# Four image layers on one core: ends of attention blocks in pieces, a first load in smaller pieces, a setup in steps

## The chip, the cores and the metric

The kernel runs on one core of a Trainium2 chip, in one launch. The metric is device time in microseconds; three runs of the kernel before give a median of 2654.44 us (2654.04 to 2654.82). A profiled execution of it spans 2652.8 us. A core has five engines that work side by side, each through its own queue in order: TensorE (PE in the profile: matrix products and transposes; PEld are its weight loads), VectorE (DVE), ScalarE (ACT), GpSimd (POOL) and SyncE (SP, which here only issues transfers). They wait for each other through semaphores. Operands lie in SBUF, products arrive in PSUM, a small memory that TensorE writes and VectorE and ScalarE read.

## The reference

The input is four images of 64 x 64 positions with 64 channels, float32 (n = 4096 positions per image). Four layers follow each other; all of them are done in float32.

```python
# layer 0: self-attention over positions; attn is used transposed
q, k, v = (x @ Wq + bq, x @ Wk + bk, x @ Wv + bv)          # each (b, n, 64)
attn = softmax(q @ k^T, axis=-1)                            # (b, n, n)
x = gamma * einsum("bmn,bmc->bnc", attn, v) + x

# layer 1: gated convolution block
y = dw3x3(layernorm(x) @ pw1 + b)                           # 256 channels
y = y1 * y2                                                 # halves of the channels
y = y * (mean(y over positions) @ sca + b)
x = x + (y @ pw2 + b) * beta
z = layernorm(x) @ pw3 + b
x = x + ((z1 * z2) @ pw4 + b) * gamma

# layer 2: attention along the other reading of the same memory, no weights
xf = x.reshape(b, 64, n)
x = softmax(xf @ xf^T) applied to xf, plus x

# layer 3: non-local block with batch norm over all images
f = softmax((x @ theta) @ (x @ phi)^T)                      # inner width 32
w_y = (f @ (x @ g)) @ w_W + w_b
out = x + gamma * (w_y - mean(w_y)) * rsqrt(var(w_y) + 1e-3) + beta
```

(In layer 2 the code writes `x.shape` as `B, C, H, W`, so it is the first image axis, of length 64, that plays the channels, and the 4096 others are the summed positions; the kernel follows that.) The mean and variance of layer 3 go over all images, so the output can't begin before the last of them has been projected.

## The kernel before

**Tiles.** `X` holds all four images in SBUF, each as 128 partitions (two halves of the image times 64 channels) by 2048 columns. PSUM is shared out as three tiles `ps` of 128 x 1024 (`new_ps`), which take scores, projections and transposes, and two tiles `acc` of 128 x 512 (`new_acc`), which gather sums over many products. Six tiles `e` of 128 x 2048 (`new_e`) hold exponentials. A tile that is asked for when all of its kind are in use waits until the oldest one has been read for the last time.

**Order.** The order on TensorE, VectorE and ScalarE is the order in which the program is written; nothing reorders it. `run()` (L1495) goes through a list of items. An item is one `scores` call of an attention layer: 32 of layer 0 per image, 32 of layer 2, 64 of layer 3. `at(i, fn)` adds a function that runs after the scores of item i: usually the `products` of an earlier item. So TensorE always has the scores of the next item to do while ScalarE forms the exponentials of the last. Two lanes, `conv` (setup of the weights, then layer 1) and `misc` (loads, projections, layer openings), are generators; each `yield us` says how long a step is counted for, and after the scores and again after the products of an item a lane takes as many steps as fit into the item's count (3.6 us, 4.6 us and 1.0 us a tick for layers 0, 2 and 3). Layer 3 of image b follows layer 2 of image b + 1.

**Start.** `fetch_x(0)` (L738) loads the first image in four transfers, two on SyncE's queue and two on ScalarE's; the small vector `bq` comes next on SyncE's queue. `fold_qk` multiplies the two query and key weights into one matrix `wq` and a bias `bqk`; `load_x(0)` (L920) turns the image by transposes (L924), eight per PSUM tile, with a copy to `X` (L925); `project0` (L971) makes `q` (L997, L1002) and `v` (L1007, L1009). Then come the scores of layer 0 (L1031).

**Setup of weights.** `setup()` (L879) folds the layer norm's gain, shift and mean into the weights of layer 1: eight one-column products (L891) and their sums, then for each of two matrices a scaling on VectorE (L901), a product with `cmat` (L902) and a copy. All of it but the first step is one lane step.

**Query step of images 1 to 3.** `project0` with "once" forms four products in a `ps` tile (L982); VectorE adds the bias to both halves (L990), 64 partitions x 1024 each, and a transfer doubles each half (L993).

**norm.** In layer 1 ScalarE squares the image (L1082), and after a `yield 4.0` TensorE averages the image and its squares over channels (L1088).

**Layer 2.** `scores(n)` (L1245) and exp with the sum of each row (L1253); `products(n)` (L1262) runs one item after its scores and needs both `acc` tiles when n is a multiple of 8.

**Layer 3.** `scores(n)` writes two `ps` tiles (L1361), ScalarE two exponentials (L1367). `products(n)` runs two items later. It multiplies `e` by `gx` into the accumulator `y` (L1389), and adds up `e` for the softmax's denominators: on VectorE into `esum` (L1383, L1385), or, where `mc % 10 == 9`, by TensorE with a matrix of ones straight into the accumulator `z` (L1378). Here n = 32 nb + mc: there are two blocks of 32 items, nb = 0 and 1. After a block, `yz` takes a copy of `y` (L1395), and `totals` adds `esum` into `z` (`sums`, L1399), inverts `z` as exp(-ln z) on ScalarE (L1410, L1411) with one Newton step on VectorE (L1412 to L1414), and scales `yz`. `close` multiplies `yz` with the output weights in a new `ps` tile (`project`, L1419), adds the bias on ScalarE (L1432) and takes statistics on VectorE (L1434). `totals` comes four items after the block's last scores (two for the second block of images 0 and 1), `close` eight. The last block of the last image has its own end, `close_last` (L1436 on).

**Output.** `finish()` (L1536) joins the statistics, scales, adds and transposes (L1607) and stores in pieces; before the last piece's copy, `check_sums` (L1635) counts on VectorE whether all sums of the softmaxes lie in a range. If not, a slower general path would run; with these inputs it doesn't.

Of the kernel before, what the change touches and what calls it, by code (L numbers as in the profile page):

```python
# [691 lines left out]
def fast_path(ctx: ExitStack, tc: tile.TileContext, a: dict, out: bass.AP, bad):  # L692
# [44 lines left out]

    def fetch_x(b, queues):  # L738
# [4 lines left out]
        for g in range(2):  # L743
            for p in range(2):
                (queues[p] if b == 0 else queues[g]).dma_start(
                    out=t[64 * p : 64 * p + 64, bass.ts(g, 8)], in_=src[p, :, bass.ts(g, 8)]
                )
# [131 lines left out]
    def setup():  # L879
# [7 lines left out]
        for i, (w_, sh, bi) in enumerate(  # L887
            ((pw1, "L1_conv_ln1_b", "L1_conv_pw1_b"), (pw3, "L1_conv_ln2_b", "L1_conv_pw3_b"))
        ):
            for r in range(2):  # L890
# [3 lines left out]
                )  # L894
            nc.vector.tensor_add(
                pwb[:, i, :], ps[:, 2 * i : 2 * i + 2], vec[:, col[bi] : col[bi] + 2]
            )

        ps = new_ps()
        for i, (w_, g) in enumerate(((pw1, "L1_conv_ln1_g"), (pw3, "L1_conv_ln2_g"))):  # L900
            nc.vector.tensor_scalar_mul(w_, w_, V(g))  # L901
            mm(ps[:, 512 * i : 512 * i + 256], cmat, w_, start=True, stop=True)  # L902
            nc.vector.tensor_copy(w_, ps[:, 512 * i : 512 * i + 256])
        for i in range(4):
# [5 lines left out]
        nc.vector.tensor_mul(resb[:, 0:1], V("L1_conv_pw2_b"), V("L1_conv_beta"))  # L910
        nc.vector.tensor_mul(resb[:, 1:2], V("L1_conv_pw4_b"), V("L1_conv_gamma"))
        yield 3.0
# [7 lines left out]
    def load_x(b):  # L920
        for g in range(2):
            ps = new_ps()
            for i in range(8):
                nc.tensor.transpose(ps[:, bass.ts(i, 128)], rows_x[b][:, 8 * g + i, :], ident)  # L924
            (nc.vector.tensor_copy if g else nc.scalar.copy)(X[:, b, bass.ts(g, 1024)], ps)  # L925
            yield 3.0
# [9 lines left out]
    def at(i, fn):  # L936
        due.setdefault(i, []).append(fn)
# [33 lines left out]
    def project0(b):  # L971
# [5 lines left out]
        for j, w in once if b else ((0, "q"), (0, "v"), (1, "q"), (2, "q"), (1, "v"), (3, "q")):  # L977
            ps = new_ps()
            if w == "once":
# [7 lines left out]
                for o in range(2):  # L987
                    own, other = slice(64 * o, 64 * o + 64), slice(64 - 64 * o, 128 - 64 * o)
                    n = bass.ts(2 * j + o, 512)
                    nc.vector.tensor_scalar_add(  # L990
                        qs[own, :, n], ps[own, :].rearrange("p (s n) -> p s n", s=2), bqk[own, :]
                    )
# [84 lines left out]
    def norm(x, y):  # L1077
# [5 lines left out]
        yield 4.0  # L1083
# [147 lines left out]
    def layer2(b):  # L1231
# [51 lines left out]
        for n in range(32):  # L1283
            items.append((lambda n=n: scores(n), 4.6))
            at(first + n + 1, lambda n=n: products(n))
# [17 lines left out]
    wys, early = {}, []  # L1303

# [44 lines left out]
    def layer3(b):  # L1349
# [3 lines left out]
        def scores(n):  # L1353
# [12 lines left out]
            for kp in range(2):  # L1366
                act(e[:, bass.ts(kp, 1024)], tiles[kp], AF.Exp)  # L1367

        def products(n):
# [4 lines left out]
            if mc % 10 == 9 or (last and n >= 62):  # L1374
                if mc == 9:
                    st["z"] = new_acc("accz")
# [330 lines left out]
```

## Time and profile before

Busy time of each engine in the 2652.8 us span:

| engine | busy us | share |
|---|---|---|
| TensorE (PE) | 2612.8 | 98% |
| ScalarE (ACT) | 1718.6 | 65% |
| VectorE (DVE) | 1348.6 | 51% |
| GpSimd (POOL) | 16.4 | 1% |

The dearest groups by line: exponentials of layer 0 (L1036) 517.1 us, of layer 2 (L1253) 517.0, of layer 3 (L1367) 496.0; the sums of layer 3 on VectorE (L1385) 490.4; the scores of layer 0 (L1031) 475.5 and layer 2 (L1245) 469.8; the products of layer 2 (L1262) 468.5 and layer 0 (L1056) 467.4; scores and products of layer 3 (L1361, L1389) 309.5 and 272.0.

Rows of a timeline give the start in us, the length, the engine, the line, the operation, output <- inputs with their shapes, the count, and in brackets the idle time of the engine before it with what ended it. Rows of the waits name engine and line, then what was waited for, the total in us, the number of times, and the longest. Ends of matmuls are modelled and overlap with the next ones; the distance from one start to the next is the safer measure. Matmuls that sit in different parts of the array run side by side, so a group's count says little of its time.

### The profile page before, as it was taken

To read this page: it belongs to the slowest core of one execution; us is meant where nothing else is said; L and a number is where in the kernel's file an instruction comes from. 1 tells how busy PE (TensorE), PEld (TensorE's weight loads), DVE (VectorE), ACT (ScalarE), POOL (GpSimd) and SP (SyncE) were. 2 spreads that over 40 slices of the span, in tenths; PEclk is the share of its full clock that TensorE was granted. 3 is DMA by queue.
4 is the path that set the end of the run, shared out by engine and by line. 5 is a ranking of instruction groups with operands and counts; after the bars stand their busy time and mean duration, and the time that the engine had idled before them with its cause. 6 is when DMAs were issued, how large, how long until landed. Compare 5 with 4: busy or idle time off the path is not lost.

```text
span 2652.8 us, 50797 instructions
## 1 busy us (share of the span) xinstructions
PE 2612.8 (98%) x22421; PEld 830.2 (31%) x22421; DVE 1348.6 (51%) x1555; ACT 1718.6 (65%) x2787; POOL 16.4 (1%) x66
## 2 busy tenths in 40 slices
PE   8999999999999999999999999999999999999998
PEld 3333233333323323333333322243322333322223
DVE  3232386633876338621672148800068600098997
ACT  4555655656566565666656668756578755578886
POOL 2000000000000000000000000000000000000000
PEclk9999999999999999999999999999999999999999
DMA  3000000001000100010010000010000010010002
GB/s 73 1 17 1 17 8 10 1 17 25 9 1 1 32 17 1 1 33 17 1 33 17 17 1 1 2 33 1 17 1 2 1 33 1 1 33 2 1 1 66
DMA packets 24282, 36.46 MB, mean 14 GB/s; under 512 B 3725, under 2 KB 12150, under 8 KB 24054
## 3 DMA queue, kind: packets, MB, share of 16 engines
q1 hardware_dynamic: 23141, 32.03, 5.5%
q8 instruction: 178, 2.92, 0.5%
q0 software_dynamic: 672, 0.56, 0.1%
q10 hardware_dynamic: 240, 0.54, 0.1%
q14 instruction: 51, 0.41, 0.1%
HBM read 4.80 MB, written 4.19 MB: 3 GB/s over the span
## 4 chain that ended last, share of the span: by engine, by line
PE 93%; DVE 4%; ACT 2%; issue 0%; DMA 0%; SPq 0%; DVEq 0%; ACTq 0%
PE acc L1056 17%; PE acc L1262 17%; PE ps L1031 17%; PE ps L1245 16%; PE ps L1361 10%; PE acc L1389 8%; PE ps L1118 2%; DVE tg L1385 2%; PE accz L1378 1%; ACT e L1253 1%; PE ps L1209 1%; PE ps L1186 1%; PE ps L1088 1%; PE ps L1340 1%; PE ps L1007 0%
## 5 line engine op out<-in xcount | busy, mean ns | idle before, releaser
L1036 ACT ACTIVATE e<-ps 128x1024 f32<-128x1024 f32 x512 | 517.1, 1025 | 338.1 <-PE ps L1031 225.8
L1253 ACT ACTIVATE e<-ps 128x1024 f32<-128x1024 f32 x512 | 517.0, 1025 | 305.0 <-PE ps L1245 304.9
L1367 ACT ACTIVATE e<-ps 128x1024 f32<-128x1024 f32 x512 | 496.0, 1022 | 85.4 <-PE ps L1361 78.3
L1385 DVE TENSOR_TENSOR tg<-tg,e 128x2048 f32<-128x2048 f32 x214 | 490.4, 2292 | 24.7 <-ACT e L1367 5.7
L1031 PE MATMUL ps<-X,q 64*64 64x512 f32 x4096 | 475.5, 599 | 7.6 <-DVE q L990 4.1
L1245 PE MATMUL ps<-ko 64*64 64x512 f32 x4096 | 469.8, 591 | 2.2 <-ACT ko L1227 1.6
L1262 PE MATMUL acc<-e,X 64*64 64x512 f32 x4096 | 468.5, 591 | 2.6 <-DVE inv L1412 1.6
L1056 PE MATMUL acc<-e,vq 128*64 128x512 f32 x2048 | 467.4, 598 | 0.0
L1063 DVE SCALAR_TENSOR_TENSOR yv<-acc,gam,yv 128x512 f32<-128x512 f32 x224 | 167.8, 750 | 322.6 <-PE acc L1056 311.7
L1157 DVE SCALAR_TENSOR_TENSOR y<-pad,vec,y 128x1024 f32<-128x1024 f32 x240 | 308.1, 1284 | 8.1 <-ACT pad L1141 1.0
L1361 PE MATMUL ps<-tg,ph 32*64 32x512 f32 x4096 | 309.5, 613 | 1.4 <-DVE tg L1329 0.5
L1389 PE MATMUL acc<-e,tg 128*32 128x512 f32 x2048 | 272.0, 603 | 1.5 <-ACT yz L1395 1.5
L1245 PEld LDWEIGHTS ps<-ko 64*64 64x64 f32 x4096 | 157.7, 132 | 288.1 <-issue 195.4
L1262 PEld LDWEIGHTS acc<-e,X 64*64 64x64 f32 x4096 | 159.1, 133 | 278.7 <-issue 263.3
L1031 PEld LDWEIGHTS ps<-X,q 64*64 64x64 f32 x4096 | 143.2, 133 | 323.7 <-issue 224.8
L1056 PEld LDWEIGHTS acc<-e,vq 128*64 128x64 f32 x2048 | 136.0, 136 | 315.1 <-issue 294.4
L1270 DVE TENSOR_TENSOR ph<-ph,acc 128x512 f32<-128x512 f32 x16 | 11.0, 688 | 379.6 <-ACT ph L1269 379.6
L1361 PEld LDWEIGHTS ps<-tg,ph 32*64 32x64 f32 x4096 | 79.5, 129 | 218.7 <-issue 143.2
L1389 PEld LDWEIGHTS acc<-e,tg 128*32 128x32 f32 x2048 | 43.5, 108 | 202.3 <-issue 196.3
L1253 ACT ACTIVATION_READ_ACCUMULATOR e<-ps 128x1 f32 x512 | 106.1, 207 | 0.0
L1036 ACT ACTIVATION_READ_ACCUMULATOR e<-ps 128x1 f32 x512 | 106.0, 207 | 0.0
L1141 ACT ACTIVATE pad<-ps,pwb 128x512 f32<-128x512 f32 x64 | 44.6, 697 | 45.7 <-PE ps L1118 39.0
(193 smaller groups left out, 939.9 us busy)
## 6 DMA issues: line engine op xcount, KB each, us to landing
xn<-t SPq DMA_DIRECT2D x64, 128.0 KB
ph<-tg SPq DMA_DIRECT2D x64, 128.0 KB
ko<-ko SPq DMA_DIRECT2D x16, 256.0 KB
xr<-in_x_dram SPq DMA_DIRECT2D x14, 256.0 KB
q<-q SPq DMA_DIRECT2D x12, 256.0 KB
out_dram<-o SPq DMA_DIRECT2D x5, 512.0 KB
out_dram<-o SPq DMA_DIRECT2D x6, 256.0 KB
xr<-in_x_dram ACTq DMA_DIRECT2D x2, 256.0 KB
```

What stands on the lines that cost most here:

```text
L1031: mm(ps[64 * c : 64 * c + 64, bass.ts(r, 512)], m.q[rows_, 128 * t + 64 * c : 128 * t + 64 * c + 64], x[rows_, bass.ts(g, 512)], start=Tru ...
L1036: act(es[g // 2][:, bass.ts(g % 2, 1024)], ps, AF.Exp, bias=SHIFT0, accum_out=zs[:, g : g + 1],)
L1056: mm(accs[g][64 * r : 64 * r + 64, :], vq, es[half][:, 1024 * g + 512 * r : 1024 * g + 512 * r + 512], start=t == 2 * p, stop=t == 2 * p + 1,)
L1063: stt((x if p == 15 else m.y)[:, cols], accs[g], gam0, (m.y if p else x)[:, cols], ALU.mult, ALU.add,)
L1157: stt(y1, win, wt, y1, ALU.mult, ALU.add)
L1245: mm(ps[64 * c : 64 * c + 64, bass.ts(r, 512)], m.ko[rows_, 128 * jb + 64 * c : 128 * jb + 64 * c + 64], m.ko[rows_, bass.ts(2 * ib + r, 5 ...
L1253: act(es[n, jb], ps, AF.Exp, bias=SHIFT2, accum_out=m.zs[:, jb, ib : ib + 1])
L1262: mm(acc[r][64 * c : 64 * c + 64, :], xw[rows_, jb, :], es[n, jb][rows_, bass.ts(c, 512)], start=jb == 0, stop=jb == 31,)
L1361: mm(tiles[kp][64 * c : 64 * c + 64, bass.ts(i, 512)], m.ph[rows_, 128 * mc + 64 * c : 128 * mc + 64 * c + 64], m.th[rows_, bass.ts(nb, 51 ...
L1367: act(e[:, bass.ts(kp, 1024)], tiles[kp], AF.Exp)
L1385: nc.vector.tensor_add(esum, esum, e)
L1389: mm(st["y"][32 * k : 32 * k + 32, :], m.gx[:, mc, :], e[:, bass.ts(k, 512)], start=mc == 0, stop=mc == 31,)
```

## The change

It has eight edits, each meant to take a wait out of TensorE's way or to spread a lump of work:

1. The first image is loaded in six transfers (quarters, quarter, half) and transposed in three steps, so that the first products can begin on its first quarter.
2. The setup of weights is cut into seven lane steps, and the work inside is regrouped: all small products, then VectorE, then both large products.
3. In the query step of images 1 to 3, the second half's bias goes to ScalarE.
4. norm yields 5.0 instead of 4.0 after the squares.
5. In layer 2 of images 2 and 3, the first products run two items after their scores instead of one.
6. Layer 3: TensorE takes the sums at mc = 13, 20 and 27 (and 29 from n = 61 on) instead of 9, 19 and 29.
7. Layer 3: at five of the eight block ends (all but the second blocks of images 0, 1 and 3), `spread` puts the end into single items: Ln and Exp in two halves each, the Newton step later, the projection in two halves that reuse the accumulator `z` instead of a `ps` tile, the bias in four pieces. In the item where `yz` is copied, the second exponential is held back until after the copy.
8. `check_sums` moves behind the last store.

```diff
+    parts = ((0, 4), (4, 8), (8, 16)), ((0, 8), (8, 16))
...
-        for g in range(2):
+        for lo, hi in parts[b > 0]:
             for p in range(2):
-                (queues[p] if b == 0 else queues[g]).dma_start(
-                    out=t[64 * p : 64 * p + 64, bass.ts(g, 8)], in_=src[p, :, bass.ts(g, 8)]
-                )
+                queues[p].dma_start(out=t[64 * p : 64 * p + 64, lo:hi], in_=src[p, :, lo:hi])
...
+        for i, (_, _, _, bi) in enumerate(folds):
             nc.vector.tensor_add(
                 pwb[:, i, :], ps[:, 2 * i : 2 * i + 2], vec[:, col[bi] : col[bi] + 2]
             )
+        for w_, g, _, _ in folds:
+            nc.vector.tensor_scalar_mul(w_, w_, V(g))
+        yield 5.0
         ps = new_ps()
-        for i, (w_, g) in enumerate(((pw1, "L1_conv_ln1_g"), (pw3, "L1_conv_ln2_g"))):
-            nc.vector.tensor_scalar_mul(w_, w_, V(g))
+        for i, (w_, _, _, _) in enumerate(folds):
             mm(ps[:, 512 * i : 512 * i + 256], cmat, w_, start=True, stop=True)
+        for i, (w_, _, _, _) in enumerate(folds):
             nc.vector.tensor_copy(w_, ps[:, 512 * i : 512 * i + 256])
...
+        yield 5.0
...
-                    nc.vector.tensor_scalar_add(
-                        qs[own, :, n], ps[own, :].rearrange("p (s n) -> p s n", s=2), bqk[own, :]
-                    )
+                    src = ps[own, :].rearrange("p (s n) -> p s n", s=2)
+                    if o:
+                        act(qs[own, :, n], src, AF.Identity, bias=bqk[own, :])
+                    else:
+                        nc.vector.tensor_scalar_add(qs[own, :, n], src, bqk[own, :])
...
             act(sq[i], x[:, bass.ts(i, 1024)], AF.Square)
-        yield 4.0
+        yield 5.0
...
-            at(first + n + 1, lambda n=n: products(n))
+            at(first + n + (2 if n == 0 and b > 1 else 1), lambda n=n: products(n))
...
-            for kp in range(2):
-                act(e[:, bass.ts(kp, 1024)], tiles[kp], AF.Exp)
+            for fn in small.get((first + n, "PE"), []):
+                fn()
+            act(e[:, 0:1024], tiles[0], AF.Exp)
+            held.append(lambda: act(e[:, 1024:2048], tiles[1], AF.Exp))
+            if not (mc == 1 and (nb or last)):
+                held.pop()()
+            for fn in small.get((first + n, "ACT"), []):
+                fn()
...
-            if mc % 10 == 9 or (last and n >= 62):
-                if mc == 9:
+            if mc in (13, 20, 27 if n < 61 else 29) or (last and n >= 62):
+                if mc == 13:
                     st["z"] = new_acc("accz")
...
                 nc.scalar.copy(st["yz"][:, 0:512], st["y"])
+                if held:
+                    held.pop()()
...
+        def project_half(nb, jj):
+            if jj == 0:
+                open_wy(nb)
+            for s in range(2):
+                k = 2 * s + jj
+                mm(
+                    st["z"][64 * s : 64 * s + 64, :], wo[32 * k : 32 * k + 32, :],
+                    st["yz"][32 * k : 32 * k + 32, 0:512], start=True, stop=True,
+                )
...
+        def spread(n):
+            nb = n // 32
+            at(first + n + 4, sums)
+            for m, kind, fn in (
+                (5, "ACT", lambda: invert(slice(0, 256))), (6, "ACT", lambda: invert(slice(256, 512))),
+                (7, "ACT", lambda: invert2(slice(0, 256))), (8, "ACT", lambda: invert2(slice(256, 512))),
+                (9, "ACT", lambda: newton(nb)),
+                (12, "PE", lambda: project_half(nb, 0)), (12, "ACT", lambda: take(nb, 0, 0)),
+                (13, "ACT", lambda: take(nb, 0, 1)),
+                (14, "PE", lambda: project_half(nb, 1)), (14, "ACT", lambda: take(nb, 1, 0)),
+                (15, "ACT", lambda: take(nb, 1, 1)),
+            ):
+                small.setdefault((first + n + m, kind), []).append(fn)
...
-                at(first + n + (2 if n == 63 and b < 2 else 4), lambda n=n: totals(n // 32))
-                at(first + n + 8, lambda n=n: close(n // 32))
+                spread(n)
...
-                check_sums(mv)
...
+        check_sums(mv)
```

## The prediction

> **What bounds the kernel now.** I read the busy shares first, then the waits of TensorE, then TensorE's timeline at each place the diff touches.
>
> ```profile
> PE 2612.8 (98%) x22421; PEld 830.2 (31%) x22421; DVE 1348.6 (51%) x1555; ACT 1718.6 (65%) x2787; POOL 16.4 (1%) x66
> PE ps L1031 <- DVE q L990: 4.1, 2, 3.1
> PE acc L1262 <- DVE inv L1412: 1.6, 2, 0.8
> PE ps L1088 <- ACT sq L1082: 1.6, 1, 1.6
> PE acc L1389 <- ACT yz L1395: 1.5, 5, 0.3
> PE acc L875 <- DMA bq<-in_L_conv_bq_dram: 1.2, 1, 1.2
> ```
>
> TensorE is the bound: 40.0 us of the 2652.8 us span are not its work. A part of the change can win only what it takes out of these 40, plus matmuls that run slowly after a gap; each matmul that it adds is paid in full. The wait rows (total, times, longest) name what the edits aim at. They are small, so each is priced in its own stretch.
>
> Timeline of TensorE in the setup of weights (start, length, count, idle before):
>
> ```profile
> 45.66 0.60 PE L891 MATMUL ps<-vec,pw 64*128 64x1 f32 x4
> 47.24 0.57 PE L891 MATMUL ps<-vec,pw 64*128 64x1 f32 x4 [0.98 <-issue]
> 48.39 0.67 PE L902 MATMUL ps<-pw,cmat 128*128 128x256 f32 x2 [0.57 <-issue]
> 49.84 0.81 PE L902 MATMUL ps<-pw,cmat 128*128 128x256 f32 x2 [0.78 <-DVE pw L901]
> 50.58 5.19 PE L1031 MATMUL ps<-X,q 64*64 64x512 f32 x32
> 55.70 0.65 PE L1056 MATMUL acc<-e,vq 128*64 128x512 f32 x2
> ```
>
> Three gaps, and then 32 matmuls in 5.12 us that take 3.59 elsewhere.
>
> The same at a block end of layer 3:
>
> ```profile
> 2476.62 1.06 PE L1389 MATMUL acc<-e,tg 128*32 128x512 f32 x8 [0.31 <-ACT yz L1395]
> 2477.62 1.11 PE L1361 MATMUL ps<-tg,ph 32*64 32x512 f32 x16
> 2478.77 1.06 PE L1399 MATMUL accz<-tg,ones 128*32 128x512 f32 x8
> 2486.94 1.63 PE L1361 MATMUL ps<-tg,ph 32*64 32x512 f32 x16
> 2488.40 1.09 PE L1419 MATMUL ps<-yz,wo 32*64 32x512 f32 x8
> 2489.41 1.07 PE L1389 MATMUL acc<-e,tg 128*32 128x512 f32 x8
> ```
>
> To see: one wait of 0.31, the sums (L1399), one scores group of 1.63 instead of 1.11, the projection (L1419) in 1.01 to the next start. Then the start of layer 2 on image 2:
>
> ```profile
> 1710.27 1.04 PE L1399 MATMUL accz<-tg,ones 128*32 128x512 f32 x8
> 1711.60 1.07 PE L1262 MATMUL acc<-e,X 64*64 64x512 f32 x2 [0.30 <-ACT yz L1395]
> 1713.49 3.23 PE L1262 MATMUL acc<-e,X 64*64 64x512 f32 x27 [0.82 <-DVE inv L1412]
> ```
>
> **What the Trainium skill says.** (1) "TensorE: Matmul & The Clock Gate", What's actually happening: the array runs at half rate until a window of about 3.4 us was busy, and falls back after an idle one. The trace agrees: after the 3.15 us gap at 400.80, the 128-column matmuls of L1007 start 0.21 us apart until 408.6, then 0.11. (2) The same page, Part 3, The mechanism: matmuls in different tiles of the array run side by side. So a group costs the length of one, however many share it: L1419 holds 4 products in 1.01 us (2488.40 to 2489.41), L1186 only 2, also in 1.01 (1152.11 to 1153.12). (3) "ScalarE: Activation LUTs", What ACT_TABLE_LOAD costs: an ACTIVATE costs 186 ns, or 280 with a bias operand, plus 0.833 ns a column, and neighbours overlap by 93 ns. The trace has 0.375 us for 256 columns (L1440), 0.60 for 512, 1.02 for 1024. Cutting one of 512 into two of 256 costs ScalarE about 0.15 us more.
>
> **The change, part by part.**
>
> Setup of weights: from 45.66 to 55.70 are 10.04 us. After: eight L891 at 0.11 with a tail, 0.95; four L902 at 0.21 warm, 0.95; scores 3.59, with no gap between, as VectorE works while other matmuls run. 10.04 − 5.49 = **−4.5**.
>
> Query step of later images (L990): the second half goes from VectorE to ScalarE. At 396.5 VectorE has two such halves (1.28 each) in its queue, one before and one as the last; with one of each gone, the slot that L1031 waits for comes some 2.0 us earlier, and the gap of 3.15 becomes 1.15. Then most of the window is busy and L1118 (1.45 to the next start, not 0.95) and ten L1007 (0.21, not 0.11) stay warm: 0.5 + 1.0. At 666.63 the other gap, 0.98, loses 0.9, since the ScalarE half (about 1.0, as a 1024-column ACTIVATE) starts at once. ScalarE is busy 4.9 of 7.2 us in such an item, so it hides the half. −4.4; I take **−4.0**.
>
> norm, yield 4 to 5: a lane tick in layer 2 is 4.6 us, so with 4.0 the squares and the matmuls that read them can fall into one tick, as at 1159.40 (gap 1.62; and the 8 matmuls take 1.93 to the next start, not 0.99, as the second square trickles in). With 5.0 the reading step comes a tick later there: **−2.5**. All later steps of layer 1 shift by about half an item, with other meetings that I can't price: bounds 0 and −2.6.
>
> First products of layer 2 one item later, on two images: from 1710.27 to the third following scores at about 1723.7 are 13.4 us, where 0.96 + 3 × 3.59 = 11.7 are work. Loss 1.7. After, ScalarE still has the copy, Ln and Exp (0.59, 0.60, 0.63) ahead of the next exps, which costs the fourth score group some 0.2. 2 × 1.5 = **−3.0**. It must hold one item more of e, 6 of 6 buffers, which just fits.
>
> Range checks behind the last store: TensorE's last group and the last copy no longer have the VectorE checks (2641.37 to 2643.57) ahead of them; the last store goes about 0.7 earlier: **−0.6**. The checks then run under the store's transfer.
>
> First image in pieces: the first transposes start about 1 us sooner, but the projection waits for bq, whose transfer stands behind the image in SyncE's queue and lands at 10.1 either way. The four transposes for columns 512 to 1023, until now done under that wait, come after it: 4 × 0.21 = 0.85 later, part of it regained under the wait for q and the clock. **+0.5**, bounds −0.5 and +2.0 (if the array warms a window later).
>
> Layer 3, sums by TensorE: before, mc = 9, 19, 29. After 13, 20, 27, and in the second block 29 as well, since at n = 59 mc is 27 and at n = 61 it is 29. That is one more z sum for each image: the item with one lasts 2.98, one without 2.12, so 4 × 0.86 = 3.4. Two waits of 0.37 for VectorE's sums (L1399) go: **+2.7**.
>
> Layer 3, block ends in pieces, on five of the ends (both of images 2, first of 0, 1 and 3): an undisturbed item takes 2.12: scores 1.04, then 1.08 in which exp of the first tile must end before the next scores' second tile has its slot. ScalarE idles about 0.18 in it, so anything longer that is put into an item without extra matmuls delays TensorE. Now an end costs, in starts of scores over 2.12 each: 0.3 (copy of y), 0.8 (sums), 0.2 (Ln, Exp, mostly under the sums), 1.3 (projection with the 0.5 of stalled scores, since VectorE sat before Ln/Exp for 3.24 us and gave e buffers back late): 2.5. After: the copy 0.3 still (held back exp or not, ScalarE has 0.5 more in that item); sums 0.8; four Ln/Exp pieces of 0.33 net in plain items, 4 × 0.15 = 0.6; two half projections of 0.86 each, for both are as long as the whole was, 1.7; two of the four takes in plain items, 0.2; and the next z sum waits some 0.25 for the last take to give the bank back: 3.85. The stall by VectorE goes. Of the new waits, a take's for its half projection (0.9 us after the scores) ends before the exps ahead of it (1.94), so nothing queued behind it is late; a half projection's for yz finds VectorE's three steps (3 × 0.69) begun three items before; the held exp has only the next item's exps behind it. 5 × 1.35 = **+6.7**. Bounds: if the pieces all hide, 5 × (0.86 − 0.65) = +1; if takes and pieces stall fully, +9.
>
> Setup's splitting of half and the held lane steps are VectorE work beside TensorE: 0.
>
> Sum: −4.5 − 4.0 − 2.5 − 3.0 − 0.6 + 0.5 + 2.7 + 6.7 = −4.7, so 2654.4 − 4.7 = **2649.7 us**.
>
> **The rivals.** (A) The pieces of the block ends hide: +1 instead of +6.7, all else as above: 2644.0. For it: ScalarE is busy 126.0 of 143.0 us in the last layer 3, so it has room on average. Against: the room comes as 0.18 per item, and the half projections are TensorE's own work. (B) The gains of the moved steps (norm, query step) are lost to new meetings, 3 us of the 6.5 left, the rest as forecast, and the start costs 1.0: 2653.7, no change. For it: VectorE's queue around 400 is full of layer 1 steps that move. (C) Slower: only setup, half the layer 2 gain and 1.5 of the query step hold (−7.5), start +2, z sums +3.4, ends +9: +6.9, 2661.3. Against it: the setup gaps can't stay.
>
> **How the numbers follow.** Forecast 0.45, A 0.27, B 0.20, C 0.08. The forecast lies at −0.18%, so about 0.4 of its chance falls beyond −0.2%: faster 0.27 + 0.18 = 0.45; within 0.2%: 0.27 + 0.20 = 0.47; slower 0.08. The range holds the forecast, A and B with the bounds of norm and start: 2642 to 2657.
>
> **What would show it.** In the profile after: no gaps around L891 and L902 and scores of 3.6 us behind them; the q wait under 1.5 us; no wait of L1262 for inv; L1378 with 240 matmuls instead of 208; two groups in place of L1419 at five ends, each near 0.9 us; plain scores with small lags where Ln, Exp and takes stand. I am wrong if a scores item with a piece stays at 2.12 us, if the half projections run under the scores, or if the start gets shorter.

## The result, and the profile after

The changed kernel takes 2668.94 us (median of 6, 2667.53 to 2669.37), the kernel before 2655.14 beside it (2654.04 to 2656.13). The ratio is 1.0051, 95% interval 1.0039 to 1.0064. So the change costs some 14 us, where 4.7 less were forecast; the time lies above the forecast's range, on the side of its third rival (2661.3) and beyond it.

The busy shares of the kernel after:

```profile
PE 2623.7 (98%) x22453; PEld 829.8 (31%) x22453; DVE 1331.3 (50%) x1545; ACT 1724.9 (65%) x2819; POOL 16.5 (1%) x66
```

The span grew by 14.0, from 2652.8 to 2666.8. TensorE is busy 2623.7 − 2612.8 = 10.9 longer, and idle 43.1 instead of 40.0. In these profiles each product stands as two matmuls, a transpose as one (so the eight matmuls of L891, called eight products above, are four products). The 32 additional matmuls are one z sum of four products on each of four images. By the lines of the two profiles the z sums take 32.6 instead of 27.7 (L1397, before L1378), and the projections 14.6 instead of 8.9 (L1465 and L1449, before L1419), since five of them now come in two halves. That makes 10.6, about the whole growth: of the other matmuls some run more slowly behind new gaps and some faster where a gap has gone, and in the sum these nearly cancel. TensorE's waits after (total, times, longest):

```profile
PE ps L1042 <- ACT q L1001: 4.2, 2, 3.5
PE ps L1374 <- DVE tg L1332: 3.7, 1, 3.7
PE acc L875 <- DMA bq<-in_L_conv_bq_dram: 3.7, 1, 3.7
...
PE ps L1328 <- DVE X L1309: 2.8, 1, 2.8
PE acc L1720 <- DVE inside L1718: 2.3, 1, 2.3
PE acc L1273 <- DVE X L1074: 2.1, 1, 2.1
PE ps L1042 <- ACT pad L1152: 2.0, 1, 2.0
```

To see: the query wait is still there, as long as before, and now names ScalarE. The wait for the squares (1.6) and the ones for `inv` (1.6) are gone, as forecast, and the one for `bq` has grown, also as forecast. Four others are new or have grown from at most 0.5: L1374 for the theta bias of layer 3's opening, L1328 for the end of layer 2, L1273 for the end of layer 0 and L1042 for layer 1's `pad`. The wait of L1720 is the range check, which now lies under the last store.

Where the time went shows in the starts of the stages. For each stage, its first scores' start in TensorE's timeline less the same start before, in us. "norm at 4" is experiment 2 below, "kept parts" experiment 9.

| stage, in order of time | after | norm at 4 | kept parts |
|---|---|---|---|
| layer 0, image 1 | −5.60 | −5.47 | −5.43 |
| layer 0, image 2 | −5.62 | −4.43 | −9.28 |
| layer 0, image 3 | −1.19 | −4.16 | −8.92 |
| layer 2, image 0 | −1.66 | −4.17 | −8.92 |
| layer 2, image 1 | −1.08 | −4.18 | −8.93 |
| layer 3, image 0 | +5.38 | −4.19 | −8.85 |
| layer 2, image 2 | +7.41 | −2.17 | −9.08 |
| layer 3, image 1 | +5.16 | −4.42 | −11.33 |
| layer 2, image 3 | +7.19 | −2.38 | −11.57 |
| layer 3, image 2 | +4.95 | −4.63 | −13.82 |
| layer 3, image 3 | +11.53 | +1.83 | −14.04 |
| end | +13.95 | +4.44 | −14.71 |

Between layer 0 of image 1 and of image 2, 1 to 2 us differ from run to run with the clock after the query gap (last section). The losses sit in four places: layer 0 of image 2 (+4.4), layer 2 of image 1 (+6.5), layer 3 of image 2 (+6.6), and 2.0 to 2.4 in each layer 3 of images 0, 1 and 3.

**The parts that held.** The setup, TensorE's timeline after:

```profile
45.06 1.05 PE L893 MATMUL ps<-vec,pw 64*128 64x1 f32 x8
46.04 3.66 PE L1042 MATMUL ps<-X,q 64*64 64x512 f32 x32
...
50.70 1.51 PE L1067 MATMUL acc<-e,vq 128*64 128x512 f32 x6
```

No gap is left, and the 32 matmuls of the scores take 3.66 instead of 5.19: the stretch is 5.64 long (45.06 to 50.70) and was 10.04, so 4.4 were won where 4.5 were forecast. The start of layer 2 on image 2, TensorE after:

```profile
1718.64 3.67 PE L1256 MATMUL ps<-ko 64*64 64x512 f32 x32
1722.13 7.05 PE L1273 MATMUL acc<-e,X 64*64 64x512 f32 x64
```

Scores stand where the products waited twice; the products of two items then run as one group without a gap. From the table this stage wins 2.25 (7.41 to 5.16, and 7.19 to 4.95), where 1.5 each was forecast.

### The profile page after: what moved, and what is told of

Read it like the earlier page. It is cut to its first block, busy times and chain, and to the rows that moved or that the text cites. A ratio compares the mean times of both kernels' runs of the same rounds, so it can differ in the third digit from the quotient of the medians.

```text
span 2666.8 us, 50869 instructions
## 1 busy us (share of the span) xinstructions
PE 2623.7 (98%) x22453; PEld 829.8 (31%) x22453; DVE 1331.3 (50%) x1545; ACT 1724.9 (65%) x2819; POOL 16.5 (1%) x66
## 3 DMA queue, kind: packets, MB, share of 16 engines
HBM read 4.80 MB, written 4.19 MB: 3 GB/s over the span
## 4 chain that ended last, share of the span: by engine, by line
PE 93%; DVE 4%; ACT 1%; DMA 0%; issue 0%; SPq 0%; POOL 0%; DVEq 0%; POOLq 0%
PE acc L1067 17%; PE ps L1042 17%; PE acc L1273 16%; PE ps L1256 16%; PE ps L1374 10%; PE acc L1408 9%; PE ps L1129 2%; DVE y L1168 1%; PE accz L1397 1%; DVE tg L1404 1%; PE ps L1018 1%; PE ps L1220 1%; PE ps L1197 1%; PE ps L1353 1%; PE ps L1099 1%; PE accz L1465 0%
## 5 line engine op out<-in xcount | busy, mean ns | idle before, releaser
L1264 ACT ACTIVATE e<-ps 128x1024 f32<-128x1024 f32 x512 | 516.6, 1024 | 299.4 <-PE ps L1256 299.3
L1047 ACT ACTIVATE e<-ps 128x1024 f32<-128x1024 f32 x512 | 516.6, 1024 | 296.7 <-PE ps L1042 209.2
L1404 DVE TENSOR_TENSOR tg<-tg,e 128x2048 f32<-128x2048 f32 x210 | 481.1, 2291 | 30.5 <-ACT e L1382 12.9
L1042 PE MATMUL ps<-X,q 64*64 64x512 f32 x4096 | 474.8, 599 | 8.7 <-ACT q L1001 4.2
L1273 PE MATMUL acc<-e,X 64*64 64x512 f32 x4096 | 467.6, 594 | 2.1 <-DVE X L1074 2.1
L1381 ACT ACTIVATE e<-ps 128x1024 f32<-128x1024 f32 x256 | 262.8, 1027 | 98.6 <-PE ps L1374 80.4
L1374 PE MATMUL ps<-tg,ph 32*64 32x512 f32 x4096 | 312.0, 615 | 4.2 <-DVE tg L1332 3.7
L1168 DVE SCALAR_TENSOR_TENSOR y<-pad,vec,y 128x1024 f32<-128x1024 f32 x240 | 308.1, 1284 | 7.5
L1382 ACT ACTIVATE e<-ps 128x1024 f32<-128x1024 f32 x256 | 261.9, 1023 | 0.0
L1273 PEld LDWEIGHTS acc<-e,X 64*64 64x64 f32 x4096 | 157.3, 134 | 280.5 <-issue 272.8
L1042 PEld LDWEIGHTS ps<-X,q 64*64 64x64 f32 x4096 | 143.5, 133 | 321.0 <-issue 218.0
L1374 PEld LDWEIGHTS ps<-tg,ph 32*64 32x64 f32 x4096 | 80.5, 130 | 221.8 <-issue 123.9
```

What stands on the lines that cost most here:

```text
L1042: mm(ps[64 * c : 64 * c + 64, bass.ts(r, 512)], m.q[rows_, 128 * t + 64 * c : 128 * t + 64 * c + 64], x[rows_, bass.ts(g, 512)], start=Tru ...
L1047: act(es[g // 2][:, bass.ts(g % 2, 1024)], ps, AF.Exp, bias=SHIFT0, accum_out=zs[:, g : g + 1],)
L1168: stt(y1, win, wt, y1, ALU.mult, ALU.add)
L1264: act(es[n, jb], ps, AF.Exp, bias=SHIFT2, accum_out=m.zs[:, jb, ib : ib + 1])
L1273: mm(acc[r][64 * c : 64 * c + 64, :], xw[rows_, jb, :], es[n, jb][rows_, bass.ts(c, 512)], start=jb == 0, stop=jb == 31,)
L1374: mm(tiles[kp][64 * c : 64 * c + 64, bass.ts(i, 512)], m.ph[rows_, 128 * mc + 64 * c : 128 * mc + 64 * c + 64], m.th[rows_, bass.ts(nb, 51 ...
```

## The experiments

Line numbers of the experiments differ by a few from those of the kernel after. The kernel before took 2654.2 to 2654.4 us (median) beside them.

**1. The query step's second half back on VectorE** (the rest as changed):

```diff
-                    if o:
-                        act(qs[own, :, n], src, AF.Identity, bias=bqk[own, :])
-                    else:
-                        nc.vector.tensor_scalar_add(qs[own, :, n], src, bqk[own, :])
+                    nc.vector.tensor_scalar_add(qs[own, :, n], src, bqk[own, :])
```

> The changed kernel with the query step as before (both halves' bias on VectorE). Kernel before about 2655.1, changed kernel 2668.9. Theory: the ScalarE half starts only when the VectorE half of the same tile has ended (waits of 2.51 and 6.27 us on q in the trace of the changed kernel), so the split never made the slot come sooner; undoing it gives 2666 to 2670, and the gap at the query step stays near 3 us. Rival: ScalarE's queue, held up by that wait, is what made the later gaps of layers 0 to 2; then this run is at 2662 or below.

Measured: 2667.29 us, ratio to before 1.0049 [1.0032, 1.0066]; the interval covers that of the changed kernel. So the split wins nothing. The reason is in the timeline after, at the query step of image 2 (all engines):

```profile
392.13 2.60 DVE L1168 SCALAR_TENSOR_TENSOR y<-pad,vec,y 128x1024 f32<-128x1024 f32 x2
...
394.65 1.27 DVE L1003 TENSOR_SCALAR q<-ps,bqk 64x1024 f32<-64x1024 f32 x1
...
395.96 1.11 ACT L1001 ACTIVATE q<-ps,bqk 64x1024 f32<-64x1024 f32 x1 [6.27 <-DVE q L1003]
...
397.12 3.69 PE L1042 MATMUL ps<-X,q 64*64 64x512 f32 x16 [3.51 <-ACT q L1001]
```

ScalarE was idle for 6.27 us, for the last 4.1 of them with its products ready (the group L991 ends at 391.89), and began 0.04 after VectorE's half ended (394.65 + 1.27 = 395.92). VectorE's half stood behind two depthwise steps of layer 1's convolution (L1168). The halves do not run side by side: the second starts when the first has ended. The same holds for all six pairs of this kernel, for which ScalarE waits 15.8 us in all. It was to be seen before, in the copies of `ko` (the same two engines, one tile, 64 partitions each), which the prediction doesn't use. The tile's view in the kernel before (least, median and largest duration in ns; first and last start):

```profile
L1227 DVE COPY ko<-ps x8: 1205/1213/1217, 909.5 to 1873.3; 64x1024 f32<-64x1024 f32 x8
L1227 ACT COPY ko<-ps x8: 1007/1007/1008, 910.8 to 1874.6; 64x1024 f32<-64x1024 f32 x8
```

The first and last copies of VectorE start at 909.5 and 1873.3, those of ScalarE 1.3 later both times, once VectorE's 1.2 are over. ScalarE's waits count 12.7 us in 7 cases for it.

**2. norm's step counted as 4 again** (the rest as changed):

```diff
             act(sq[i], x[:, bass.ts(i, 1024)], AF.Square)
-        yield 5.0
+        yield 4.0
```

> The changed kernel with the yield of 4.0 after the squares of norm. Theory: the 5.0 moves every later step of layer 1 by half an item or more, and the new gaps at 739.5 (ScalarE pad), 1050.4 (VectorE X) and 1334.7 us (opening of layer 3 of the first image) come from these meetings; together with the cold matmuls behind them some 13 us, less the 3.6 us that the 5.0 won at the one wait it was for: 2658 to 2661, those three gaps gone, the old gap of 1.6 us back. Rival: the gaps come from the query split; then within 2 us of 2668.9.

Measured: 2659.70 us, 1.0019 [1.0012, 1.0027]; one number in the list of steps costs 9.2 us. In the kernel after, the meeting it was made for is gone: TensorE goes from L1099 on `X` (1165.67) to L1099 on `sq` (1166.56) without a gap. But every later step of layer 1 stands elsewhere. Layer 0 of image 2, all engines after:

```profile
736.08 1.41 DVE L1171 SCALAR_TENSOR_TENSOR yg<-pad,vec,y 128x512 f32<-128x512 f32 x2
...
737.81 0.21 POOL L1144 MEMSET pad<- 128x64 f32 x1
738.05 1.41 ACT L1152 ACTIVATE pad<-ps,pwb 128x512 f32<-128x512 f32 x2 [5.21 <-POOL pad L1144]
...
739.52 2.69 PE L1042 MATMUL ps<-X,q 64*64 64x512 f32 x16 [1.97 <-ACT pad L1152]
```

`pad` is free only after VectorE's last depthwise step, GpSimd clears it, ScalarE fills it, and the exponentials wait behind that in ScalarE's queue. Then the end of layer 0 and the opening of layer 3 during layer 2 of image 1, VectorE and TensorE after:

```profile
1041.78 7.88 DVE L1168 SCALAR_TENSOR_TENSOR y<-pad,vec,y 128x1024 f32<-128x1024 f32 x6
...
1049.58 1.40 DVE L1074 SCALAR_TENSOR_TENSOR X<-acc,gam,yv 128x512 f32<-128x512 f32 x2
...
1050.38 5.58 PE L1273 MATMUL acc<-e,X 64*64 64x512 f32 x29 [2.13 <-DVE X L1074]
```

```profile
1330.71 2.60 DVE L1168 SCALAR_TENSOR_TENSOR y<-pad,vec,y 128x1024 f32<-128x1024 f32 x2
...
1333.95 0.69 DVE L1309 TENSOR_TENSOR X<-X,ph 128x512 f32<-128x512 f32 x1
```

```profile
1334.70 1.87 PE L1328 MATMUL ps<-X,thw 64*32 64x512 f32 x4 [2.80 <-DVE X L1309]
1336.50 4.48 PE L1273 MATMUL acc<-e,X 64*64 64x512 f32 x32
```

Six depthwise steps stand ahead of the last residual of layer 0, and two stand between the last steps of layer 2's end. After this last gap the 32 matmuls of L1273 take 4.48 instead of the 3.61 of an undisturbed group. Stretches of that place (from : to, length, TensorE's busy time and matmuls, granted clock as a share of full speed, DMA share, GB/s):

```profile
1326.00:1331.00 5.00, 4.98 (x46) 1.00 0.00 0
1331.00:1334.70 3.70, 0.90 (x5) 1.00 0.00 0
1334.70:1337.00 2.30, 2.30 (x8) 0.52 0.00 0
```

The gap is paid twice, once as idle time and once as half clock after it. The Trainium skill's page "TensorE: Matmul & The Clock Gate", What's actually happening, gives an idle window of about 3.4 us as what drops the clock; the half clock of 0.52 agrees, but here a gap of 2.80 was enough, so a gap below that figure isn't safe (a longer one, 3.1, didn't always bring it; see the last section). All three gaps are gone in this experiment (its rows: L1042 for `pad` 0.4, L1273 for `X` 0.3, none for L1328).

**3. The sums rule alone** (the kernel before, with the new positions):

```diff
-            if mc % 10 == 9 or (last and n >= 62):
-                if mc == 9:
+            if mc in (13, 20, 27 if n < 61 else 29) or (last and n >= 62):
+                if mc == 13:
```

> The kernel before with only the new rule of which items TensorE sums (13, 20, 27 and in the second block 29). Theory: four more z sums of 0.86 us, and at the opening of layer 3 for the last image VectorE, without the relief of item 9, comes 3.3 us later with the step that the scores wait for, with cold matmuls behind it, 5 us: 2663 to 2664.5. Rival 1: only the sums: 2658.5. Rival 2: VectorE's relief is worth as much as the sums cost: 2655.

Measured: 2662.97 us, 1.003 [1.0018, 1.0041], so some 8 us where 2.7 were forecast. Layer 3 of images 0 and 1 loses 0.78 each in this trace, as one more z sum does; layer 3 of image 2 loses 6.1. The wait is the same as in the kernel after (3.73 in both). All engines in the kernel after, in layer 3 of image 2, where the opening of layer 3 of the last image falls:

```profile
2353.99 7.08 DVE L1404 TENSOR_TENSOR tg<-tg,e 128x2048 f32<-128x2048 f32 x3
...
2354.62 1.92 PE L1328 MATMUL ps<-X,thw 64*32 64x512 f32 x16
...
2360.99 1.28 DVE L1332 TENSOR_SCALAR tg<-ps,vec 128x1024 f32<-128x1024 f32 x1
...
2362.32 2.02 PE L1374 MATMUL ps<-tg,ph 32*64 32x512 f32 x16 [3.73 <-DVE tg L1332]
```

The same place before:

```profile
2353.64 1.28 DVE L1319 TENSOR_SCALAR tg<-ps,vec 128x1024 f32<-128x1024 f32 x1
...
2354.97 1.12 PE L1361 MATMUL ps<-tg,ph 32*64 32x512 f32 x16 [0.48 <-DVE tg L1319]
```

Without the sum on TensorE at mc = 9, VectorE has one addition of 2.29 more in its queue, just where it also ends layer 2 and opens layer 3. The theta bias L1332 then comes 4.45 after its products (2360.99 − 2354.62 − 1.92) instead of 1.2 after them, and it holds a `ps` slot that the scores need. Of these 3.3 more, about 2.3 are the addition; the rest is TensorE, which comes there some 0.9 sooner when it has no sum to do.

**4. The block ends in two lumps as before** (the rest as changed):

```diff
             elif n % 32 == 31:
-                spread(n)
+                at(first + n + (2 if n == 63 and b < 2 else 4), lambda n=n: totals(n // 32))
+                at(first + n + 8, lambda n=n: close(n // 32))
```

and the exponential isn't held back.

> The changed kernel with the block ends of layer 3 as before (totals four items after a block, close eight after, no held exponential), all else as changed. Theory: each of the five ends in pieces costs about 1.2 us more than in one lump (two half projections as long as the whole one each, small ScalarE steps in full items): 2662 to 2664. Rival: the pieces hide and the lumps bring their stalls back: 2669 to 2671.

Measured: 2662.66 us, 1.0031 [1.002, 1.0043], 6.3 less than the changed kernel by the medians; by the traces layer 3 of images 0 and 1 loses 1.24 to 1.26 per end more with the pieces. All of layer 3 loses 4.9 more by the traces; in this experiment's trace the matmuls behind the gap in image 2 stayed slow for 1.15 longer, and without that it would be some 6.1. The end in the last layer 3, TensorE after:

```profile
2488.84 1.61 PE L1374 MATMUL ps<-tg,ph 32*64 32x512 f32 x16
...
2492.22 1.11 PE L1374 MATMUL ps<-tg,ph 32*64 32x512 f32 x16
...
2507.09 1.21 PE L1374 MATMUL ps<-tg,ph 32*64 32x512 f32 x16
2508.00 1.15 PE L1465 MATMUL accz<-yz,wo 32*64 32x512 f32 x4
...
2510.08 1.11 PE L1374 MATMUL ps<-tg,ph 32*64 32x512 f32 x16
...
2513.63 1.07 PE L1465 MATMUL accz<-yz,wo 32*64 32x512 f32 x4 [0.19 <-ACT wy L1472]
...
2515.63 1.11 PE L1374 MATMUL ps<-tg,ph 32*64 32x512 f32 x16
```

From one scores to the next: 3.38 in the item with the sums, 2.99 with the first half projection, 3.51 with the second (from 2512.12), 2.12 undisturbed; and the item with the next z sum, 2517.67 to 2520.99, takes 3.32 instead of 2.98, for it waits for the last take. Together 1.26 + 0.87 + 1.39 + 0.34 = 3.86 over plain items, where 3.85 was forecast. A half projection of two products (four matmuls) lasts 1.07 to 1.15, and before the whole one of four took 1.09: that a half costs as much as the whole, as the prediction said, holds. The second half also waits 0.19 until its accumulator is free. The Ln and Exp pieces, on the other hand, cost TensorE nothing. Each takes ScalarE 0.39 to 0.44, and between the scores of 2492.22 and those of 2502.85 lie five items, 10.63 in all or 2.13 each, with all four pieces in them. The wait for the copy of `y` (1.5 in five waits before) is gone too, but the copy's 0.58 on ScalarE has only moved: the exponentials behind it come later, and in the next item, the one with the sums, the scores take 1.61 instead of 1.11.

**5. Setup in steps, first products one item later, check behind the store, on the kernel before** (the three edits as in the change, nothing else).

> The kernel before with only three of the edits: setup in steps, first products of layer 2 one item later on images 2 and 3, range checks behind the last store. Theory: these are the parts that win, 4.4 + 2 x 2.2 + 0.8 as read from the starts of items in the traces: 2644 to 2647 against 2654 to 2655 before. Rival: the setup's other lane times or the fuller buffers cost elsewhere what they win: 2650 or more.

Measured: 2645.87 us, 0.9968 [0.9957, 0.9979]. Together these three win 8.3, about what the prediction gave them (−4.5 − 3.0 − 0.6 = −8.1). By the trace: −5.3 by item 8 of layer 0, −2.24 in each later layer 2, −0.2 at the end. Another −1.6 in layer 0 of image 1 belongs to no edit: in this execution the clock did not fall after the query gap (last section).

**6. The same, and the query split with ScalarE's half written first:**

```diff
-                for o in range(2):
+                for o in (1, 0):
```

> The last kernel with the query step split as in the change, but the ScalarE half written first. Theory: the two halves run one after the other because they share tiles, in the order in which they are written; with ScalarE first, its half runs at once and VectorE's queue holds one operation of 1.28 us instead of two. The gap of 3.15 us becomes 1.2 to 1.5, and cold matmuls behind it fall away: 2.5 to 4 us below the last kernel. Rival: VectorE now waits for ScalarE and nothing is won: within 1 us of the last kernel, or above it.

Measured: 2641.09 us, 0.9952 [0.9936, 0.9969], 4.8 less than experiment 5 by the medians (2.5 by the traces, since the profiled execution of experiment 5 had kept its clock and stood 2.8 under its median). The intervals of the two experiments overlap, their runs do not (2643.03 to 2647.21 against 2640.54 to 2642.31). The query step in its timeline:

```profile
391.40 1.11 ACT L999 ACTIVATE q<-ps,bqk 64x1024 f32<-64x1024 f32 x1 [4.75 <-PE ps L989]
...
393.82 1.09 PE L1040 MATMUL ps<-X,q 64*64 64x512 f32 x8 [0.77 <-ACT e L1045]
394.22 1.27 DVE L1001 TENSOR_SCALAR q<-ps,bqk 64x1024 f32<-64x1024 f32 x1
...
395.55 1.09 PE L1040 MATMUL ps<-X,q 64*64 64x512 f32 x8 [0.64 <-DVE q L1001]
```

The free engine goes first and the busy one second. In this pair VectorE's half starts late because VectorE is busy; in the other five it starts within 0.1 of the end of ScalarE's, and VectorE stands idle for up to 7.7 us for it, which costs nothing here. The gap of 3.1 has become 0.77 + 0.64, and the clock stays at 1.00 behind it. So the split's idea was good for roughly what the prediction gave it (−4.0), and the order in which the halves are written undid it.

**7. One whole projection in a tile of its own, with one bias step** (experiment 2 with this in place of the two halves):

```diff
-                (12, "PE", lambda: project_half(nb, 0)), (12, "ACT", lambda: take(nb, 0, 0)),
-                (13, "ACT", lambda: take(nb, 0, 1)),
-                (14, "PE", lambda: project_half(nb, 1)), (14, "ACT", lambda: take(nb, 1, 0)),
-                (15, "ACT", lambda: take(nb, 1, 1)),
+                (12, "PE", lambda: whole(nb)), (12, "ACT", lambda: whole_out(nb)),
```

> The changed kernel with norm at 4.0 (2659.7) and with the projection at a block end in one piece of four products in a tile of its own, and one bias step, twelve items after the block; Ln, Exp and Newton in pieces as changed. Theory: a half projection lasts as long as the whole, so each of five ends gets some 1.0 us back (0.86 of TensorE, and the wait of the next sums for the last bias piece): 2654 to 2656. Rival: the tile of its own stalls the scores as much as the second half costs: 2659 to 2661.

Measured: 2652.06 us, 0.9992 [0.9984, 1.0001], 7.6 less than experiment 2 and below what either theory expected. That is 1.5 per end, about the price of what is gone, the second half projection (1.39) and the wait of the next z sum for the last take (0.34). Which share the single bias step has in it was not tried.

**8. Three sums per block again, the first at mc = 9 on image 2** (experiment 2 with this in place of the new rule):

```diff
-            if mc in (13, 20, 27 if n < 61 else 29) or (last and n >= 62):
-                if mc == 13:
+            ones_at = (9 if b == 2 and nb == 0 else 13, 20, 29 if nb else 27)
+            if mc in ones_at or (last and n >= 62):
+                if mc == ones_at[0]:
```

> The changed kernel with norm at 4.0 (2659.7), where TensorE takes three sums a block (none more at n = 59), and for the first block of image 2 the first of them at item 9. Theory: the stall at the opening of layer 3 for the last image (3.7 us and 1.5 us of cold matmuls) goes, and so do three of four extra sums' 0.8 us (the last one was free): 2651 to 2653. Rival: the stall is not VectorE's backlog of sums and stays: 2657.

Measured: 2651.35 us, 0.9988 [0.9981, 0.9995], 8.35 less than experiment 2: 0.8 for each sum taken out on images 0 and 1, 0.7 at the end, and 5.05 in layer 3 of image 2. The scores behind the theta bias there:

```profile
2348.25 1.12 PE L1374 MATMUL ps<-tg,ph 32*64 32x512 f32 x16 [0.48 <-DVE tg L1332]
```

0.48, as before the change. This tells the two causes of experiment 3 apart: the stall comes from the place of one sum, not from their number. (On image 2 this experiment changes the number as well, but the sum that it takes out, at n = 59, comes after the stall.)

**9. The parts that hold, together:** experiment 6 with the block ends of experiment 7, norm at 4, the old sums rule, and the first image in two parts.

> The change with five things altered: the norm step's cost back at 4, the query split kept but ScalarE's half written ahead of VectorE's, the sums rule as before the change (every tenth step), the projection of a block end whole in a tile of its own with one bias step, and the first image in two parts as before. My theory (the costs found so far add up): the run with setup, check and split alone took 2641.1 us; five block ends at about 0.3 us less each than the lump give 2639.5, range 2637.5 to 2641.5. Rival: the ends in pieces shift the layer-2 and layer-3 steps of the next image and lose what they save, 2642 to 2646.

Measured: 2639.9 us, 0.9944 [0.9927, 0.9961]: 14.5 less than before. It beats both kernels. Against experiment 6 only 1.2 by the medians and 0.6 by the traces come from the ends, which is within the noise.

**10. The same with norm at 5.**

> The previous kernel with the norm step's cost at 5 again, as in the change. Theory 1 (the 9.2 us came from the hand-overs that one more item of norm made in the change, and each of these depends on where the other steps land): the loss differs from 9.2, somewhere between 3 and 10, time 2643 to 2650, with new gaps ahead of scores of layer 1 or ahead of the opening of layer 2 or 3 as in the change. Rival (the norm step at 5 is good in itself, it lost only beside the half projections and the later sums): no slower than the previous kernel, 2636 to 2640.

Measured: 2648.5 us, 0.9977 [0.9968, 0.9986]: 8.6 more. Its waits hold the same three gaps as the changed kernel's, with the same lengths: 2.8, 2.1 and 2.0. The cost of the later step thus does not hang on the half projections or on the sums. By the busy times of the two profiles it is half gaps and half slower products: the span grows by 9.5 (2638.1 to 2647.6), TensorE's busy time by 4.9 (2606.7 to 2611.6).

**11. The first image's parts alone, on the kernel before.**

> The kernel before with the first image's smaller parts and the second loading step ahead of the loop, nothing else. My theory (the split lets no product start sooner, since the weights' arrival and the next step's wait take its place): 0.3 to 1.3 us slower than before, 2654.7 to 2655.7 beside 2654.3. Rival (the prediction's step: about 0.5 us either way, mostly a gain when the first scores no longer wait for the second half): 2652 to 2654.

Measured: 2656.45 us, 1.0007 [1.0000, 1.0014], so some 2 slower by the estimate, with an interval from 0 to 3.7. TensorE's start in it, and then in the kernel before:

```profile
5.66 1.09 PE L924 MATMUL ps<-ident,xr 128*128 128x128 f32 x4 [0.98 <-DMA xr<-in_x_dram]
10.11 0.58 PE L875 MATMUL acc<-bq,qkt 64*128 64x1 f32 x2 [3.37 <-DMA bq<-in_L_conv_bq_dram]
```

```profile
6.93 1.94 PE L924 MATMUL ps<-ident,xr 128*128 128x128 f32 x8 [2.11 <-DMA xr<-in_x_dram]
10.10 0.58 PE L875 MATMUL acc<-bq,qkt 64*128 64x1 f32 x2 [1.23 <-DMA bq<-in_L_conv_bq_dram]
```

The first transposes start 1.27 earlier and `bq` lands at the same time, so the saving turns into a longer wait (3.37 for 1.23) and twelve transposes come behind it instead of eight, as the prediction said. In the trace the first scores then start 0.1 later and item 8 of layer 0 0.5 later, but experiment 3, which leaves layer 0 alone, is 0.35 late there too; and another 0.9 stand after the query gap of image 2, where experiment 3 has 1.1. So the trace doesn't tell the edit's cost from what differs between executions. It agrees with the forecast of 0.5 and doesn't prove it; the times allow 0 to 3.7.

## Why the prediction was wrong, step by step

| step | forecast | measured | from |
|---|---|---|---|
| setup in steps | −4.5 | −4.4 | timeline after |
| query step | −4.0 | 0 to +2 | experiment 1 |
| norm at 5 | −2.5 | +9.2 | experiment 2 |
| layer 2, first products | −3.0 | −4.5 | table of stages |
| check behind the store | −0.6 | −0.2 | experiment 5 |
| first image in pieces | +0.5 | 0 to +2 | trace and time of experiment 11 |
| sums rule | +2.7 | +8 | experiments 3, 8 |
| block ends | +6.7 | +4.9 to +6.3 | traces, experiment 4 |
| sum | −4.7 | about +13 to +18 | measured as a whole: +13.8 |

The single values were taken in different surroundings, each with an uncertainty of 1 to 3, and don't add up exactly.

Three steps failed; they hold more than the 18.5 us between forecast and result, since layer 2 gave back 1.5:

- **norm.** The step read "All later steps of layer 1 shift by about half an item, with other meetings that I can't price: bounds 0 and −2.6". What I couldn't price was left out of the bounds. The wait I counted was won (1.62, and the slow products behind it), and three others of 2.0, 2.1 and 2.8, each with a slow stretch, were made. With norm the difference is 11.7.
- **Query step.** "since the ScalarE half (about 1.0, as a 1024-column ACTIVATE) starts at once" is what failed. It was written of the smaller gap, but the price of the larger one rests on it too. Its size was right (1.11), its start wasn't: it waited for VectorE's half, the very one that stands behind the layer 1 steps. That the gap comes from what VectorE has in its queue was right; the split as written leaves VectorE's half there and puts ScalarE's behind it. The difference is 4 to 6.
- **Sums rule.** The extra sums were about right (0.78 each on images 0 and 1 against 0.86; the last image's cost 0.1 in experiment 3 and 0.7 in experiment 8). The step overlooked what the sum at mc = 9 does besides: it spares VectorE 2.29 at the one place where VectorE sets the pace. The difference is some 5.

The block ends were right in the sum (1.0 to 1.3 each against 1.35) and partly wrong inside: the pieces of Ln and Exp, priced at 0.6 per end, cost nothing, and the second half projection with its takes cost 1.4. Items with such a piece stay at 2.13, which the prediction had named as a sign that it is wrong. One slip of adding stands in it too: the parts of an end before (0.3, 0.8, 0.2, 1.3) make 2.6 and not 2.5, so its own terms give 1.25 per end, or 6.2 for five. Rival A, that the pieces hide, was therefore right for ScalarE and wrong for TensorE. Rival B had the mechanism of norm, new meetings, but let them take back only what the moved steps win. Rival C named the right side, but for other reasons: it had setup, half the layer 2 gain and part of the query gain hold, while z sums and ends lost more. Layer 2's step was right and its size was 0.75 too small each time, on the good side.

Two things stay open. No experiment tells which tile makes one half of the query step wait for the other: `ps`, which both read, or `q`, which both write. A place in the traces speaks for `ps`: when the second image is turned before the change, ScalarE copies into `X` from 143.41 to 144.44 and VectorE from 143.84 to 145.07, so two engines do write parts of one tile at once when they read two different `ps` tiles. The Trainium skill's page "PSUM — Partial Sum Buffer", PSUM bank collisions raise a hardware error, says that two engines may access one bank at the same time if they are in different quadrants of 32 partitions, and that those in the same one have to be kept apart. The two halves have 64 partitions each and share no quadrant, so as far as the page goes they could overlap; in the traces none of them does. So an order that the program keeps, and not the chip, is the likely cause, but this is argued and not shown: the wait itself was not taken away in any run. And whether another step count for norm, or a shift of the depthwise steps along with it, would keep the 3.2 to 3.5 that layer 2 of image 0 gains at that place (experiments 2 and 10) without the three new gaps was not tried.

## What to carry to other kernels

A step that is moved in a list of steps moves everything behind it: before you count its gain, look for the places where another engine's queue stands just short of setting the pace (here VectorE at the end of layer 0, of layer 2, and at the opening of layer 3), and put their loss into the range even if you can't say which of them will be hit. When two engines share a tile, find in the trace whether such pairs overlap; if they don't, write the half of the idle engine first (the one time it was tried here it won 2.5 to 4.8 us). A sum that one engine takes over from another should be valued at the place where it stands and not by the average load.

## What the runs showed of the hardware that was not expected

- VectorE's and ScalarE's halves of one `ps` tile ran strictly one after the other, with 0.04 us between them (VectorE's end 395.92, ScalarE's start 395.96), in either order of writing.
- In the kernel after, TensorE's gaps of 2.0 to 3.7 us were followed by products that took up to 1.8 times as long (2.02 for the scores after the gap at 2362.32, 1.11 elsewhere), at a granted clock of 0.52 in the stretch after a gap of 2.80, and of 0.62 from 742.00 to 745.00, behind the one of 1.97. From experiment 9 to 10 the slow products cost as much as the gaps themselves (4.9 and 4.6).
- What a gap of one and the same length costs in clock differs between executions. The query step of image 2 has a gap of 3.1 us in experiments 3 and 5 (both without an edit to it). Stretches of TensorE in experiment 3, and then in experiment 5:

```profile
400.00:404.00 4.00, 1.09 (x8) 0.90 0.00 0
404.00:408.00 4.00, 3.71 (x17) 0.50 0.66 135
```

```profile
396.00:400.00 4.00, 1.38 (x16) 1.00 0.38 78
400.00:404.00 4.00, 4.00 (x32) 1.00 0.28 57
```

In the first the clock falls to 0.50 behind the gap, in the second it stays at 1.00. The starts of the stages behind it differ by 2.7 from that (1.1 later than before in one, 1.6 earlier in the other). The Trainium skill's section cited for the clock ("TensorE: Matmul & The Clock Gate", What's actually happening) calls the window free-running, so that the cost of a gap would depend on where it falls in the window. The two stretches fit that, but no run shows the window itself.
